# One decoder layer, self attention: the product of weights and values as four 32-column tiles of the array, one per head, with four batches in a group and one copy out of PSUM

## The chip, the cores and the metric

The kernel runs on one core of a Trainium2 chip. The core has five engines that run side by side and wait for one another through semaphores: TensorE (matrix products; PE in the profile, with its weight loads as PEld), VectorE (DVE), ScalarE (ACT), GpSimd (POOL) and SyncE (SP), which here only issues DMAs. Products come out in PSUM, in banks [...], and a DVE or ACT instruction has to copy them to SBUF.

The metric is the device time of one execution in microseconds (us). Three runs of the kernel before took 1482.58, 1488.05 and 1488.45 us; the median, 1488.05, is the time before. Shorter is better.

## What is computed

A decoder layer for 16 batches of 100 tokens, width 512: causal self attention with 16 heads of 32, a residual and a layer norm; cross attention to 361 encoder tokens; a layer of eight experts. The change touches the end of the self attention only:

```python
score = jnp.einsum('bhqd,bhkd->bhqk', q, k) * scale
score = jnp.where(mask, -jnp.inf, score)
attn = jax.nn.softmax(score, axis=-1)
o = jnp.einsum('bhqk,bhkd->bhqd', attn, v)
o = o.transpose(0, 2, 1, 3).reshape(b, s, H)
return o @ w_o.T
```

The line with `attn, v` is the one that is computed in another way. For one batch and one head it is a product of 100x100 weights with 100x32 values.

## The kernel before

**Tiling.** The 16 batches are taken in four groups `g` of `GB` = 4 batches; `r` is the batch in its group. The 512 columns (16 heads) are taken in four chunks `c` of 128 columns, which are four heads; `j` is the head in its chunk. An item is one `(g, c, r)`: four heads of one batch. There are 64 items, and 16 pairs `(g, c)`.

**Work of an item.** `self_scores` (L323) makes the scores of four heads in one bank (three products in float32r, since a float32 number is held as a pair of float32r numbers: `mm3`, L129), adds the mask and takes the minimum on DVE (L332), takes the exponential on ACT (L350, or L343 and L346), and scales by the inverse sum on POOL (L360). `self_turn` (L367) transposes the four 100x100 blocks with TensorE (L372) into a bank of tag `t`, and ACT copies them to `pT` (L374), so that the key token is on the partitions. `self_attend` (L376) then multiplies: the stationary operand is `v`, 100 key tokens by the 128 columns of the chunk; the moving operand is all of `pT`, 100 by 400 (four heads side by side). This product is in float32. Its result `av` is 128x400, and of every head's 100 columns only the 32 rows of that head are wanted, a diagonal of four 32x100 blocks. Four copies bring these blocks to `O`, on DVE (L389) or on ACT (L391). After the fourth batch a DMA on SP's queue writes `O` to DRAM (L393), from where the output projection `b_load` reads it later.

**Order.** A loop over the 64 items (L475 to L482) calls `self_attend` of item i, then what `extra` puts there (the projections of the next chunk: `self_q`, `self_k`, `self_v`, each 12 products; weight loads; the first tiles of the output projection), then the scores of item i + 3 and the transposes of item i + 1. A scheduler takes these calls and sets each engine's final order by a timeline of its own; buffers of pools set what can be in flight: `v` has 6, `pT` has 2, `av` has 2 banks.

**After it.** The output projection and the queries of the cross attention follow (`b_out`, `b_q`). The queries' weights `wq_2` and `wq_3` are loaded near the end of the self attention into the arena slots of the self attention's own weights; their DMAs (L189) stand on SP's queue behind the output DMA (L393) of the last group.

Of the kernel before, what the change touches and what calls it, by code (L numbers as in the profile page):

```python
# [17 lines left out]
B, S, D = 16, 100, 512  # batches, tokens of a batch, model width  # L18
T = B * S
KC = D // 128  # chunks of the model width  # L20
NH = 16  # heads of both attentions
HD1 = D // NH  # head width of the self attention
SE = 361  # encoder tokens of a batch
SP = SE + 1  # the same, even
NKV, HD2 = 4, 128  # key/value heads and head width of the cross attention
GR = NH // NKV
CH = [(0, 128), (128, 128), (256, SE - 256)]  # chunks of the encoder tokens
NE = 8  # experts
GB = 4  # batches of a token group
NG = B // GB  # L30
GT = GB * S
TT = [(t, min(128, T - t)) for t in range(0, T, 128)]  # tiles of all tokens
# [5 lines left out]
def pieces(t0, n):  # L38
    """The batches that tokens t0 to t0 + n lie in: (batch, its token, offset, count)."""
    out, t = [], t0  # L40
    while t < t0 + n:
        b, r = divmod(t, S)
        m = min(S - r, t0 + n - t)
        out.append((b, r, t - t0, m))
        t += m
    return out


class Pair:
    """A float32 array as the exact sum of two that float32r holds."""  # L50
# [12 lines left out]
def tile_decoder_layer(  # L63
# [29 lines left out]
    # Exp and Ln of one table serve both attentions.  # L93
# [25 lines left out]

    def split(dst, src, high=None, low=None):  # L120
        """dst, a pair, from src."""
        high, low = high or nc.scalar, low or nc.vector
        if high is nc.scalar:
            nc.scalar.copy(dst.h, src)  # L124
        else:
            high.tensor_copy(dst.h, src)
        low.tensor_tensor(dst.l, src, dst.h.bitcast(FP), ALU.subtract)  # L127

    def mm3(out, a, b, start, stop):  # L129
        """The product of two pairs, to float32's accuracy."""  # L130
        nc.tensor.matmul(out, a.h, b.h, start=start, stop=False)  # L131
        nc.tensor.matmul(out, a.h, b.l, start=False, stop=False)  # L132
        nc.tensor.matmul(out, a.l, b.h, start=False, stop=stop)  # L133
# [5 lines left out]
    def rsqrt(v, p, n, name, p_=None):  # L139
        """1 / sqrt(v), from the activation tables, with one Newton step."""  # L140
# [33 lines left out]
    # Eight slots of 512 rows by 512 columns, each a pair: weights, and what fits  # L174
    # beside them.
# [9 lines left out]
    def split_rows(dst, src, name, high=None, low=None):  # L185
        """Weights from DRAM into a pair, by rows."""
# [48 lines left out]
    def chunk(n, c, queue=None):  # L235
        """Weights from DRAM, 128 columns (of queries or keys) or rows (of values)."""
# [18 lines left out]
    # Keys of four heads, each in its own block of rows and of columns.  # L255
# [8 lines left out]
    # Added to negated scores: zero up to the diagonal, BIG past it.  # L264
# [25 lines left out]
    def self_v(g, r):  # L290
# [6 lines left out]
        V[g, r] = w1.tile([S, D], FP, name=f"v_{g}_{r}", tag="v", bufs=6)  # L297
        nc.scalar.copy(V[g, r], pv)

    def self_q(g, c):  # L300
# [3 lines left out]
        # The scores come out negated and scaled.  # L304
# [62 lines left out]
    def self_turn(g, c, r):  # L367
# [5 lines left out]
        PT[g, c, r] = w2.tile([S, 4, S], FP, name=f"pT_{n}", tag="pT")  # L373
        nc.scalar.copy(PT[g, c, r], pt)  # L374

    def self_attend(g, c, r):  # L376
        n = f"{g}_{c}_{r}"
        cols = slice(r * S, (r + 1) * S)
        pT = PT.pop((g, c, r))
        # Of each head's rows only its own columns are its output.  # L380
        av = bank("av", [128, 4, S], f"av_{n}")
        v = V[g, r][:, c * 128 : (c + 1) * 128]
        nc.tensor.matmul(av, v, pT, start=True, stop=True)  # L383
        if r == 0:
            O[g, c] = w2.tile([128, GT], FP, name=f"o_{g}_{c}", tag="o")
        for j in range(4):
            rows = slice(32 * j, 32 * j + 32)
            if j == 3 or (j == 1 and r % 2 == 0):
                nc.vector.tensor_copy(O[g, c][rows, cols], av[rows, j, :])  # L389
            else:  # L390
                nc.scalar.copy(O[g, c][rows, cols], av[rows, j, :])  # L391
        if r == GB - 1:
            nc.sync.dma_start(o1d[g][:, c], O[g, c])  # L393

# [34 lines left out]
    LA = 3  # items that scores are ahead by  # L429
    extra = {}  # what comes with an item  # L430
# [44 lines left out]
    for i, it in enumerate(items):  # L475
        self_attend(*it)
# [4 lines left out]
        if i + 1 < len(items):  # L481
            self_turn(*items[i + 1])  # L482
    a_l.close()

# [23 lines left out]
    # Both norms' weights and the negated scale of the scores.  # L508
# [107 lines left out]
    # Six pairs of values and two of queries, in slots 1 and 5.  # L616
# [87 lines left out]
    def x_attend(b, g, i):  # L704
# [13 lines left out]
        # The weights of a token sum to one: the values' bias comes last.  # L718
# [27 lines left out]
    TAIL = 3  # tiles whose parts come by weights, not by tiles  # L746
# [12 lines left out]
    def d_part(i, among={}):  # L759
        """A part of the output's product; others' products are among its own."""  # L760
        t, g = parts[i]
        n = TT[t][1]
        if g == 0:
            # The scores' banks are free by the time that those of the first wait.
# [28 lines left out]
    HEAD = 1  # parts with a group of heads of the last batch  # L793
# [51 lines left out]
    # Small products: logits, ranks, counts, tokens of slots, their experts.  # L845
# [30 lines left out]
    def d_logits(t):  # L876
        """The products of the router with a tile, to go among longer ones."""
# [15 lines left out]
    # An expert's tokens in order, 128 to a tile of slots. The tiles of slots come in  # L893
    # the order in which their first tokens do, but the first EARLY of those that the
    # tokens of the first CUT tiles fill come before the others.
    URGENT = 1000
    I32, HF = mybir.dt.int32, mybir.dt.float16
    NSL = NE + (2 * T - NE) // 128  # tiles of slots: enough for any choice
    CUT, EARLY = NT - 4, 11
    # At the cut at most NE - 1 tiles' worth of choices lies in tiles not full.  # L900
# [9 lines left out]
    # Whole numbers below 2 ** 11 are in float16 where products take them.  # L910
    # Expert numbers less NE, negative ones.
# [5 lines left out]
    # Ones where the partition's number comes before the column's.  # L917
# [11 lines left out]
    # lower[e, i] is one where i is less than e, on all partitions.  # L929
# [31 lines left out]
    def by_128(dst, src, name):  # L961
        """The whole part of src / 128."""
# [5 lines left out]
    def table(name, shape, dt=FP):  # L968
        """A table of shape, first after partitions the tiles."""
# [3 lines left out]
    def choose(a, b):  # L973
        """The two experts of each token of tiles a to b, and its ranks in them."""
# [4 lines left out]
        for j in range(2):  # L979
            # The largest value of each token, and the first place that has it.  # L980
# [19 lines left out]
        if b == NT:  # L1000
            # The last tile's tokens past the end choose none.
# [17 lines left out]
        if b in (CUT, NT):  # L1019
            # The choices that come before each tile of tokens.  # L1020
# [26 lines left out]
        # What the tokens give to their slots: the tile's expert, by its first slot,  # L1047
# [7 lines left out]
        # and their numbers.  # L1055
# [11 lines left out]
    def settle(a, b):  # L1067
        """The tiles of slots of the choices of tiles a to b."""
# [6 lines left out]
        # Tiles of slots that an expert has before each tile of tokens.  # L1075
# [4 lines left out]
        # One where it opens another.  # L1080
# [5 lines left out]
        def before_it(these, till, less, name):  # L1086
            """How many of these come before each."""
# [28 lines left out]
        # That one's place among all tiles of slots.  # L1116
        new = before_it(opn, opened, EARLY if a else 0, "new")
        if a == 0:
# [6 lines left out]
            # new less those of the first EARLY that come before it, negated,  # L1125
# [3 lines left out]
            # or first, if it is itself of those.  # L1129
# [6 lines left out]
        # The place of the one before it.  # L1136
# [7 lines left out]
        # The tile of slots of a choice, by its rank.  # L1144
# [18 lines left out]
    def slots(a, b, upto):  # L1163
        """Of tiles a to b of slots: the tokens, and where the weights lie."""
# [69 lines left out]
    early = [1, 2, 5, 6]  # slots that are free already  # L1234
# [117 lines left out]
    # Tiles of tokens from REST on come after the last product, from LATE on also  # L1352
    # the gathers for them.
    REST, LATE = 6, 8
    # When the tiles before LATE are turned to, by tiles of slots.
    TURN = (19, 20, 21, 22, 24, 26, 28, 30)
    BEHIND = 2  # products that the last norms come after

    def upto(t):
        """Tiles of slots among which are all that the tokens of tile t are in."""  # L1360
        # At most NE of the tiles so far are not full at the cut.
# [93 lines left out]
    # Roots taken together: of tiles in the first norm, of tiles in the second.  # L1455
# [16 lines left out]
    def root(j, t, of=V2):  # L1472
        """What to take the root of for tile t in norm j, or its reciprocal root."""
# [8 lines left out]
    def f_first(t):  # L1482
        """The first norm of tile t, and what the second takes."""
# [3 lines left out]
        # The first norm's result and x2, both times the root s: the second norm  # L1487
        # drops s, but for its share of v.
# [62 lines left out]
    def roots(v, m, name):  # L1551
        """Of v's first m columns the root of four times it, of the others 1 / sqrt."""
# [6 lines left out]
        # A Newton step for each.  # L1559
# [15 lines left out]
    def newton(v, name):  # L1575
        """1 / sqrt(v): from a guess by v's exponent, three Newton steps."""
# [130 lines left out]
```

## Time and profile before

The profiled execution has a span of 1484.0 us, from its first instruction to its last; some 4 us lie around it when it is set beside the median of 1488.05 us. The self attention takes the first 257 us of the span.

| in the first 257 us of the span | instructions | busy us | mean ns of one |
|---|---|---|---|
| TensorE, all products | 1194 | 239.3 | |
| product av (L383) | 128 | 56.1 | 534 |
| transposes pt (L372) | 256 | 32.9 | 257 |
| VectorE, all | 835 | 177.9 | |
| ScalarE, all | 626 | 183.5 | |
| GpSimd, all | 159 | 140.4 | |
| ScalarE copy pT (L374), 100x400 | 64 | 30.6 | 487 |

How to read it: a float32 product of the program shows as two products, each with a weight load of its own, so the 64 products at L383 are 128 rows; a transpose shows as one, so four transposes for each of the 64 items are 256 rows. The mean duration of a product is not its price, since products are pipelined: a product lasts until its last result is out, while the next has long begun. The price is the distance between starts, and the chain of waits shows it. Busy times of different engines lie beside each other and are not to be added.

### The profile page before, as it was taken

The page shows a single profiled execution, that of the slowest core. Times are in us where ns is not written, and L with a number is a line of the kernel's source. Part 1 is how long each engine was busy: PE and PEld are TensorE (multiplying, and loading weights), DVE is VectorE, ACT ScalarE, POOL GpSimd, SP SyncE. Part 2 cuts the span into 40 slices and gives each one's busy share as a digit, 9 for nine tenths or more (in the row PEclk, how much of TensorE's full clock was granted, in tenths as well). Part 3 has the DMA queues.
Part 4 walks back from the last instruction along what each step waited for, and adds up shares of the span by engine and source line. Part 5 has one row for each costly group of instructions (what it writes and reads, how often), then busy time and mean ns, then how long its engine had stood idle before and what let it go on. Part 6 is the DMA issues. An engine that isn't in the chain of part 4 may idle for free.

```text
span 1484.0 us, 24770 instructions
## 1 busy us (share of the span) xinstructions
PE 1391.4 (94%) x7248; PEld 1139.8 (77%) x7248; DVE 1018.2 (69%) x3523; ACT 813.3 (55%) x2164; POOL 731.9 (49%) x853
## 2 busy tenths in 40 slices
PE   7999999999999999999999999999999898798985
PEld 6777786788877888788788788788887676576763
DVE  5775766677676777777777677677745558752698
ACT  5766877444444566566666566566654233332453
POOL 6455545534424555455655555555544444442643
PEclk9999999999999999999999999999999999899997
DMA  4011015456544222122322322321435645666774
GB/s 130 34 46 62 22 36 145 144 142 118 125 97 92 74 65 80 44 64 64 89 61 64 87 63 63 93 60 45 99 107 142 207 164 159 191 213 184 253 232 146
DMA packets 197875, 159.77 MB, mean 108 GB/s; under 512 B 133322, under 2 KB 152878, under 8 KB 197742
## 3 DMA queue, kind: packets, MB, share of 16 engines
q1 hardware_dynamic: 187904, 137.83, 33.7%
q0 software_dynamic: 4576, 14.95, 3.3%
q10 hardware_dynamic: 5262, 5.41, 1.3%
q8 instruction: 60, 0.98, 0.3%
q14 instruction: 73, 0.60, 0.1%
HBM read 107.16 MB, written 50.99 MB: 107 GB/s over the span
## 4 chain that ended last, share of the span: by engine, by line
PE 67%; DVE 17%; DMA 7%; issue 4%; ACT 3%; POOL 1%; SPq 1%; DVEq 0%; POOLq 0%; ACTq 0%
PE pv L131 4%; PE pv L132 4%; PE pv L133 4%; PE pq L131 4%; PE ptp L700 4%; PE pq L132 4%; PE pq L133 3%; PE s L131 3%; PE s L133 3%; PE s L132 3%; PE pk L131 3%; PE pk L133 3%; PE pk L132 3%; DVE ksq L639 2%; PE av L383 2%
## 5 line engine op out<-in xcount | busy, mean ns | idle before, releaser
L692 POOL TENSOR_SCALAR p<-p,sums 100x361 f32<-100x361 f32 x256 | 146.7, 577 | 107.7 <-DVE sums L691 88.7
L679 DVE CUSTOM_DVE_ANT_0 p<-s,nmask 100x361 f32<-100x361 f32 x256 | 133.5, 527 | 73.6 <-PE s L133 71.5
L690 ACT ACTIVATE p<-p,nm 100x361 f32<-100x361 f32 x256 | 153.4, 602 | 47.2 <-DVE nm L679 44.1
L127 DVE TENSOR_TENSOR pT_l<-ptp,pT_h 128x400 fp32r<-128x400 f32 (+1 forms) x192 | 107.4, 567 | 58.3 <-ACT pT_h L124 58.1
L124 ACT CAST pT_h<-ptp 128x400 fp32r<-128x400 f32 (+1 forms) x192 | 91.5, 488 | 33.4 <-PE ptp L700 32.8
L700 PE MATMUL ptp<-ident,p 100*128 100x100 f32 (+1 forms) x768 | 108.2, 253 | 0.1
L700 PEld LDWEIGHTS ptp<-ident,p 100*128 100x128 f32 (+1 forms) x768 | 95.9, 152 | 15.5 <-POOL p L692 4.2
L127 POOL TENSOR_TENSOR cT_l<-cf,cT_h 128x512 fp32r<-128x512 f32 (+1 forms) x48 | 54.4, 1134 | 97.2 <-ACT cT_h L124 95.9
L133 PE MATMUL acc<-WH,ot_l 128*128 128x512 f32 (+1 forms) x208 | 86.2, 415 | 8.4 <-DVE ot_l L127 5.4
L131 PE MATMUL acc<-WH,ot_h 128*128 128x512 f32 (+1 forms) x208 | 85.8, 413 | 3.5 <-ACT ot_h L124 3.5
L127 POOL TENSOR_TENSOR WL<-qf,WH 128x400 fp32r<-128x400 f32 x64 | 67.3, 1051 | 43.5 <-ACT WH L124 39.7
L131 PE MATMUL s<-kT_h,WH 128*100 128x362 f32 x256 | 88.7, 357 | 0.0
L131 PE MATMUL av<-pT_h,WH 128*128 128x400 f32 (+1 forms) x192 | 76.7, 400 | 8.2 <-ACT pT_h L124 8.2
L132 PE MATMUL acc<-WL,ot_h 128*128 128x512 f32 (+1 forms) x208 | 84.4, 406 | 0.0
L133 PE MATMUL s<-kT_h,WL 128*100 128x362 f32 x256 | 84.1, 329 | 0.0
L132 PE MATMUL s<-kT_l,WH 128*100 128x362 f32 x256 | 83.7, 327 | 0.0
L131 PE MATMUL pq<-WH 128*128 128x512 f32 (+1 forms) x208 | 82.3, 396 | 0.1
L132 PE MATMUL pq<-WL,WH 128*128 128x512 f32 (+1 forms) x208 | 81.6, 394 | 0.5 <-POOL WL L127 0.5
L551 POOL TENSOR_TENSOR qs<-qs,r_q 128x512 f32<-128x512 f32 (+1 forms) x52 | 54.3, 1075 | 54.5 <-DVE r_q L155 25.5
L131 PE MATMUL pv<-WH,cT_h 128*128 128x512 f32 (+1 forms) x192 | 80.3, 418 | 0.8 <-DVE WL L127 0.8
L639 DVE CUSTOM_DVE_ANT_0 ksq<-ks 128x128 f32<-128x128 f32 (+1 forms) x192 | 78.3, 408 | 2.4
L360 POOL TENSOR_TENSOR p<-p,rinv 100x400 f32<-100x400 f32 x64 | 54.2, 855 | 51.8 <-DVE rinv L359 37.3
(349 smaller groups left out, 4407.3 us busy)
## 6 DMA issues: line engine op xcount, KB each, us to landing
qf<-qd SPq DMA_DIRECT2D x64, 200.0 KB, 2.6
of<-od SPq DMA_DIRECT2D x48, 256.0 KB, 3.5
cf<-in_ctxT SPq DMA_DIRECT2D x16, 722.0 KB, 4.2
eb<-in_expert_b SPq DMA_DIRECT2D x32, 256.0 KB, 3.8
ysd<-xs SPq DMA_DIRECT2D x32, 256.0 KB, 4.1
f_e<-in_expert_w SPq DMA_DIRECT2D x30, 256.0 KB, 4.5
f_wq<-in_Wq SPq DMA_DIRECT2D x16, 256.0 KB, 4.0
f_wo<-in_Wo SPq DMA_DIRECT2D x16, 256.0 KB, 4.6
```

The source lines that it names most:

```text
L124: nc.scalar.copy(dst.h, src)
L127: low.tensor_tensor(dst.l, src, dst.h.bitcast(FP), ALU.subtract)
L131: nc.tensor.matmul(out, a.h, b.h, start=start, stop=False)
L132: nc.tensor.matmul(out, a.h, b.l, start=False, stop=False)
L133: nc.tensor.matmul(out, a.l, b.h, start=False, stop=stop)
L360: nc.gpsimd.tensor_tensor(p, p, rinv.unsqueeze(2).to_broadcast([S, 4, S]), ALU.mult)
L551: nc.gpsimd.tensor_tensor(qr[:, hs, :], qr[:, hs, :], rs[:n, hs].unsqueeze(2).to_broadcast([n, GR, HD2]), ALU.mult,)
L639: nc.vector.tensor_tensor_reduce(out=sq[:n], in0=kr[:, h, :], in1=kr[:, h, :], scale=1.0, scalar=0.0, op0=ALU.mult, op1=ALU.add, accum_out ...
L679: nc.vector.tensor_tensor_reduce(out=p, in0=sc[:, :SE], in1=nmask, scale=1.0, scalar=BIG, op0=ALU.add, op1=ALU.min, accum_out=nm,)
L690: nc.scalar.activation(p, p, AF.Exp, bias=nm, scale=-1.0, accum_out=sh)
L692: nc.gpsimd.tensor_scalar(p, p, sh, 1.0, ALU.mult, ALU.mult)
L700: nc.tensor.transpose(pt[:n, h, :], probs[h][:, c0 : c0 + n], ident[:S, :S])
```

## The change

`self_attend` is no longer called for an item but once for a pair `(g, c)`, after the last batch's item. It makes 16 products, one for each batch and head, each with a stationary operand of 32 columns (that head's values) and a moving operand of 100 columns (that head's weights). `tile_position=(0, 32 * j)` places head `j` in the array's columns 32j to 32j + 31, and its result falls on partitions 32j to 32j + 31 of the bank, in the columns of its batch. The bank then holds the output as it is wanted, and one ACT copy of 128x400 takes it to `o`; the DMA is unchanged. The last batch comes first in the order of the products, and `in_turn` fixes that order for the scheduler; it adds no wait on a semaphore. `v` gets 8 buffers and `pT` 6, since weights of four batches are kept until the fourth is there. In the loop the call moves behind the extras, the scores and the transposes.

```diff
+    def in_turn(ins, prev):
+        if prev is not None:
+            tc.add_manual_dep(
+                ins.ins, prev.ins.name,
+                mybir.DependencyInfo(
+                    mybir.DependencyClass.NoSync, mybir.DependencyReason.DATA
+                ),
+                reason="in_turn",
+            )
+        return ins
...
-        V[g, r] = w1.tile([S, D], FP, name=f"v_{g}_{r}", tag="v", bufs=6)
+        V[g, r] = w1.tile([S, D], FP, name=f"v_{g}_{r}", tag="v", bufs=8)
...
-        PT[g, c, r] = w2.tile([S, 4, S], FP, name=f"pT_{n}", tag="pT")
+        PT[g, c, r] = w2.tile([S, 4, S], FP, name=f"pT_{n}", tag="pT", bufs=6)
...
-    def self_attend(g, c, r):
-        n = f"{g}_{c}_{r}"
-        cols = slice(r * S, (r + 1) * S)
-        pT = PT.pop((g, c, r))
-        av = bank("av", [128, 4, S], f"av_{n}")
-        v = V[g, r][:, c * 128 : (c + 1) * 128]
-        nc.tensor.matmul(av, v, pT, start=True, stop=True)
-        if r == 0:
-            O[g, c] = w2.tile([128, GT], FP, name=f"o_{g}_{c}", tag="o")
-        for j in range(4):
-            rows = slice(32 * j, 32 * j + 32)
-            if j == 3 or (j == 1 and r % 2 == 0):
-                nc.vector.tensor_copy(O[g, c][rows, cols], av[rows, j, :])
-            else:
-                nc.scalar.copy(O[g, c][rows, cols], av[rows, j, :])
-        if r == GB - 1:
-            nc.sync.dma_start(o1d[g][:, c], O[g, c])
+    def self_attend(g, c):
+        av = bank("av", [128, GB, S], f"av_{g}_{c}")
+        prev = None
+        for r in (GB - 1, *range(GB - 1)):
+            pT = PT.pop((g, c, r))
+            for j in range(4):
+                h = c * 128 + 32 * j
+                ins = nc.tensor.matmul(
+                    av[32 * j : 32 * j + 32, r, :],
+                    V[g, r][:, h : h + 32],
+                    pT[:, j, :],
+                    start=True,
+                    stop=True,
+                    tile_position=(0, 32 * j),
+                )
+                prev = in_turn(ins, prev)
+        o = w2.tile([128, GT], FP, name=f"o_{g}_{c}", tag="o")
+        nc.scalar.copy(o, av.rearrange("p r s -> p (r s)"))
+        nc.sync.dma_start(o1d[g][:, c], o)
...
     for i, it in enumerate(items):
-        self_attend(*it)
         for f in extra.get(it, []):
             f()
         if i + LA < len(items):
             self_scores(*items[i + LA])
         if i + 1 < len(items):
             self_turn(*items[i + 1])
+        if it[2] == GB - 1:
+            self_attend(*it[:2])
```

Comments and docstrings are also gone from the changed file, which moves its line numbers and nothing else.

More of the change, by code (lines that the diff above doesn't have):

```diff
@@ L118, in pair @@
         )
+    def in_turn(ins, prev):
+        if prev is not None:
+            tc.add_manual_dep(
+                ins.ins,
+                prev.ins.name,
+                mybir.DependencyInfo(
[4 more added lines that the diff above has]
+        return ins
     def split(dst, src, high=None, low=None):
```

## The prediction, made before the changed kernel was run

> **What bounds the kernel now.** First the engines' busy times on the page, then the chain of waits over the stretch that the change touches, then single pieces of that chain, then the groups of the lines concerned.
>
> ```profile
> PE 1391.4 (94%) x7248; PEld 1139.8 (77%) x7248; DVE 1018.2 (69%) x3523; ACT 813.3 (55%) x2164; POOL 731.9 (49%) x853
> ...
> PE 67%; DVE 17%; DMA 7%; issue 4%; ACT 3%; POOL 1%; SPq 1%; DVEq 0%; POOLq 0%; ACTq 0%
> ```
>
> TensorE is busy 94% of the span, and two thirds of the chain that ended last run on it. What it saves mostly arrives at the end; what the others save counts only where the chain passes through them. The same chain, asked for the first 257 us alone, begins so:
>
> ```profile
> by line: PE av L383 12.4%; PE pv L131 5.8%; PE pv L132 5.4%; PE pt L372 5.3%; PE pv L133 5.2%; issue 4.7%; DVE p L332 4.2%; PE pk L131 4.2%; DVE WL L127 4.1%; PE pk L133 3.8%; PE pk L132 3.8%; PE s L131 3.3%; DMA f_wq<-in_Wq 3.3%; PE pq L13
> ```
>
> The product to be changed is its largest line: 12.4% of 257 us, 31.8 us. What one product costs shows in the chain's pieces near 240 us (start, length, what):
>
> ```profile
> 239.75 0.69 PE pt L372 x8
> 240.44 0.26 PE pa L133
> 240.69 1.36 PE av L383 x4
> 242.05 0.02 issue
> 242.07 0.23 ACT o L391
> ...
> 246.77 1.72 PE pt L372 x8
> 248.49 2.71 PE av L383 x4
> ...
> 255.42 5.67 DMA f_wq<-in_Wq
> ```
>
> Two products, four rows of 400 columns, take 1.36 us: 0.34 a row, 0.68 a product. Eight transposes, float32 rows of 100 columns, take 0.69: 0.086 a row. So a row's price follows its moving columns (0.85 ns each). At 246.77 the same work takes twice as long; the granted clock of 246.6 to 253.4 us is 0.51. The copies:
>
> ```profile
> L391 ACT COPY o<-av 32x100 f32<-32x100 f32 x160 | 36.7, 232 | 30.3 <-PE av L383 21.5 <-DVE o L389 6.9
> L389 DVE COPY o<-av 32x100 f32<-32x100 f32 x96 | 24.8, 262 | 21.5 <-ACT o L391 18.9 <-PE av L383 0.6
> L374 ACT COPY pT<-pt 100x400 f32<-100x400 f32 x64 | 30.6, 487 | 1.3 <-PE pt L372 0.7
> ```
>
> A copy costs 232 to 262 ns for 100 elements a partition, and 487 ns for 400: four times the columns for twice the price.
>
> **The products.** All counts are per pair (g, c), of which there are 16. Before: 4 products at 0.68, 2.72 us. After: 16 products of 100 columns, each of two rows, so 32 rows. The moved columns are 32 x 100 = 3,200, as many as 8 x 400 before. One after another they save nothing: 32 x 0.086 = 2.75 us. The gain hangs on tiles that run at the same time, and no row of this trace shows a column tile. The cases:
>
> - All four tiles at once: 4 batches x 2 rows x 0.086 = 0.69 us. But 32 weight loads must be made too. The nearest row is the router's product at L884, which loads 128 columns for only 8 moving ones: eight such rows take 0.95 us of which the last result's 0.26 are its tail, so 0.1 us a load, 0.025 for 32 columns, 0.80 us for all 32. The loads bind: 0.80.
> - In pairs: rows start in program order, which is high part then low part of one head, then the next head's. A head's low part has to follow its high part in the same tile; the next head's high part is another tile and can run beside it. So each product costs one row and not two: 16 x 0.086 + 0.086 = 1.46.
> - One after another: 2.75.
> - One after another with loads uncovered: 32 x (0.086 + 0.025) = 3.55.
>
> Here the Trainium skill has rules for both sides. "TensorE: Matmul & The Clock Gate", Part 3 (The mechanism, and Measured speedup vs the span model), says that packed tiles start about 4 ns apart, a column packing of three measuring 2.38 times; by that rule alone the four tiles cost 0.69 + 16 x 0.004 = 0.75. The same section says that weight loads overlap running products only when row groups differ. Column tiles share all rows, so by that rule the loads lie bare, the fourth case. The trace speaks against this second rule: the transposes also use the same rows, load 100 columns each (0.08 us by the row above) and still start every 0.086 us, not every 0.17. The same section also says that products start and end in strict order, and that is what gives pairs. I take the pairs, since the high and low halves of a float32 product are adjacent in the built program's order on TensorE, and keep 0.80 and 3.55 for the ends.
>
> To each comes entering and leaving the tiled form. "TensorEngine Tiling (Array Packing)", Key Properties, says that a change of mode drains the array, with no price; the nearest row is how long a product outlasts its pace, 0.50 (its median duration) less 0.34, 0.16 us. Twice, 0.33; nothing if the drain is hidden. The built order keeps the 16 products together at nearly all 16 places (one transposition group or one score product cuts in at two), so two switches each. Sums: 1.13, 1.79, 3.08, 3.88 us against 2.72. Times 16: -25.4, -14.9, +5.8, +18.6.
>
> Of the 64 x 0.68 = 43.5 us now spent, 31.8 lie on the chain, 73%. A saving counts in that share: -18.6 or -10.9. A loss I count whole, because work that grows comes onto the chain.
>
> **The copies.** 256 go (36.7 + 24.8 = 61.5 us busy), 16 of 128x400 come at 0.49, 7.8 us, on ACT. Adding the chain's pieces on these lines gives 3.0 us for ACT and 2.9 for DVE, 5.9 of 61.5 busy. The same tenth of 7.8 remains, 0.8: -5.1 us on the chain. The rest of the 54 us saved is beside TensorE's work and gives nothing. Behind each new copy, ACT's next instructions (exponentials, pT copies) queue 0.49 where up to three old copies took 0.7, so that is no loss.
>
> **What is late next.** The first product of a group waits for the last batch's pT. In the built order, 12 projection rows or a few scores and transposes lie between at most places; in the last two groups only four transposes, 0.35 to 0.45 us against ACT's 0.49 copy: about 0.5 us in all. Then the queries' weights: their loads stand on SP's queue behind the output DMA of group (3, 2), take 5.67 us at 255.42, and pass ACT and POOL before TensorE may use them; in the trace TensorE already waits for them near 262 and 264 us. Products that get there up to 1 us sooner only wait longer: 1 us. Together +1.5. More buffers for v and pT take waits away that the list of waits prices at nearly nothing. SP's 16 output DMAs are the same, the POOL work too, and the later stages' built order is the old one but for a few swaps near the end, which I cost at nothing.
>
> **Sum.** -10.9 - 5.1 + 1.5 = -14.5 us: span 1484.0 to 1469.5. With the 4 us around it, which is the median's offset from the span, **1473.5 us**.
>
> **The rivals.**
>
> - *All four tiles run at once.* For it speaks the span rule; against it the order of high and low halves. -18.6 - 5.1 + 1.5 = -22.2: 1466.
> - *The tiles run one after another* (the change doesn't do what it says). For it: column counts are equal, and the switches cost. +5.8 - 5.1 + 1.5 = +2.2: 1490, no change that can be told.
> - *Loads lie bare in the tiled form, slower.* One mechanism, one place, the 16 runs of 32 rows: each row waits for its own load. +18.6 - 5.1 + 1.5 = +15: 1503. It decides as soon as a row costs more than (2.72 - 0.33) / 32 = 0.075 us plus what the copies give back, 3.6 us / 512 rows = 0.007, so from 0.082. One after another with covered loads stands just past that point.
>
> **How the numbers follow.** Chances: pairs 0.48, all at once 0.25, one after another 0.14, bare loads 0.13. What no case holds is the clock: three half-clock stretches (3.4, 6.8 and 6.8 us) lie in the self attention, and one more or less of 6.8 moves the time by 3.4. With it the pairs reach from 1466 to 1482. The range, 1460 to 1495, takes in the pairs, nearly all of four at once and most of one after another. About 0.5% (1480.6 to 1495.5) is what a measurement of this kernel can tell from no change. Faster by more: 0.85 of the pairs, nearly all of the second case, a tenth of the third, 0.66 in all; same 0.20; slower 0.14, bare loads and a little of the third.
>
> **What would show it.** In the changed profile the new product's line should have 512 rows, and a run of 32 should take about 1.5 us on the chain: 0.8 says all at once, 2.8 one after another, 3.5 bare loads. In the window of the first 257 us ACT's busy time should fall by about 29 us and DVE's by 25, and the first product of the queries should start about 15 us before its 254.7. The prediction is wrong if the runs of 32 are as long as the four products were, if TensorE's new idle time meets half-clock stretches, or if the softmax takes the place of the product on the chain, so that shorter runs leave the same start of the queries.

## The result, and the profile after

Four runs of the changed kernel took 1467.66 to 1474.53 us, median **1472.76 us**, beside 1486.59 us for the kernel before (four runs): ratio 0.9911, 95% interval 0.9889 to 0.9933. The forecast was 1473.5. The profiled execution's span is 1472.8 us (before 1484.0). Comments that left the file and a new helper move the lines: what was L372, L374 and L360 is now L385 (transposes), L387 (copy to `pT`) and L373 (scaling of `p`); the product is L398, the copy out L408.

The groups by line and shape, in the first 257 us (busy us, mean ns of one | idle time just before, and what ended it):

```profile
L398 PE MATMUL av<-pT,v 100*32 100x100 f32 x512 | 16.3, 267 | 2.6 <-ACT pT L387 2.6
L408 ACT COPY o<-av 128x400 f32<-128x400 f32 x16 | 7.8, 488 | 7.7 <-PE av L398 7.6
```

The 512 rows and 16 copies are there as counted. What the product costs is read from starts, not from the mean of 267 ns. TensorE's timeline (start us, length us, what), at a place without idle time:

```profile
200.96 0.35 PE L146 MATMUL s<-WH,qT_l 128*100 128x400 f32 x1
201.24 0.89 PE L398 MATMUL av<-pT,v 100*32 100x100 f32 x32
202.06 0.55 PE L385 MATMUL pt<-ident,p 100*100 100x100 f32 x4
```

From the start of the score row before to that of the transposes after are 1.10 us. The score row itself takes 0.18 (its neighbours start 0.18 apart), so the run of 32 rows costs 0.92 us, where the four products cost 2.72. Its 31 distances between starts are, in ns:

```
7, 7, 6, 91, 6, 6, 7, 66, 7, 6, 7, 65, 8, 6, 7, 65, 8, 6, 6, 67, 7, 5, 8, 65, 7, 6, 8, 65, 7, 6, 7
```

Four rows start within 20 ns, and the next four some 86 ns after the first of these (111 the first time), which is the price of one 100-column row. **All four tiles run at once**: 0.65 us from the first start to the last, then 0.18 until the next row, and some 0.1 more than usual at the entry. Twelve of the 16 runs take 0.64 to 0.65 us from first start to last; in two other work cuts in, and two ran in part or whole while the granted clock was 0.5 (1.12 and 1.19 us).

Did the saved time arrive? The first product of the queries (128x512, on TensorE) starts at 242.58 us, before it was 254.71. The busy times of the engines up to these two points (length of the window, then busy us of each engine, granted clock, share of the DMA engines, GB/s), after and before:

```profile
core 0: us, PE busy (x) PEld busy (x) DVE busy (x) ACT busy (x) POOL busy (x), PEclk, DMA share, GB/s
0.00:242.58 242.58, 210.40 (x1568) 176.86 (x1569) 154.28 (x738) 156.44 (x486) 147.29 (x164) 0.95 0.24 75
```

```profile
0.00:254.71 254.71, 236.97 (x1184) 189.57 (x1185) 177.20 (x832) 181.54 (x621) 138.13 (x157) 0.97 0.21 66
```

TensorE is busy 26.6 us less, and idle 32.2 instead of 17.7 us. So of 26.6 us saved, 12.1 arrived, and 14.4 became idle time. Behind this point the kernel takes as long as before: 1230.2 us to the end of the span, before 1229.3. The same two windows, each cut at 200 us, show where:

```profile
0.00:200.00 200.00, 180.52 (x1306) 153.25 (x1307) 126.35 (x614) 128.46 (x401) 117.66 (x135) 0.97 0.19 61
200.00:242.58 42.58, 29.88 (x264) 23.62 (x263) 27.94 (x125) 27.98 (x86) 29.64 (x30) 0.83 0.48 141
```

```profile
0.00:200.00 200.00, 184.66 (x926) 148.86 (x927) 135.77 (x623) 138.27 (x466) 110.16 (x127) 0.97 0.19 60
200.00:254.71 54.71, 52.31 (x260) 40.71 (x259) 41.43 (x212) 43.27 (x155) 27.97 (x31) 0.94 0.30 88
```

Up to 200 us TensorE is idle 19.5 us (before 15.3); in the tail, from there to the first query product, 12.7 of 42.6 us (before 2.4 of 54.7). About 4 of the 14 us lie in the first stretch and 10 in the tail. TensorE's timeline there:

```profile
226.12 0.89 PE L398 MATMUL av<-pT,v 100*32 100x100 f32 x32 [0.25 <-ACT pT L387]
230.46 0.55 PE L385 MATMUL pt<-ident,p 100*100 100x100 f32 x4 [3.45 <-POOL p L373]
231.28 0.77 PE L385 MATMUL pt<-ident,p 100*100 100x100 f32 x4 [0.26 <-POOL p L373]
236.97 0.91 PE L385 MATMUL pt<-ident,p 100*100 100x100 f32 x4 [4.92 <-POOL p L373]
...
240.32 1.56 PE L398 MATMUL av<-pT,v 100*32 100x100 f32 x32 [1.59 <-ACT pT L387]
```

The brackets hold the idle time ahead of a row and its releaser. The last items' weights (`p`) come late from GpSimd, which waits for DVE's sums of the exponentials. ScalarE's timeline shows one reason:

```profile
225.58 0.88 ACT L387 COPY pT<-pt 100x400 f32<-100x400 f32 x2
230.53 0.62 ACT L137 CAST WH<-f_wq 128x512 fp32r<-128x512 f32 x1 [4.07 <-DMA f_wq<-in_Wq]
...
232.46 0.53 ACT L359 ACTIVATE p<-p 100x400 f32<-100x400 f32 x1
...
239.26 0.62 ACT L137 CAST WH<-f_wq 128x512 fp32r<-128x512 f32 x1 [5.10 <-DMA f_wq<-in_Wq]
239.78 0.49 ACT L387 COPY pT<-pt 100x400 f32<-100x400 f32 x1
```

ScalarE stands 4.07 and 5.10 us at casts of the queries' weights, whose transfers have not landed; behind the first stands the last item's exponential, behind the second the last copy of `pT`, for which the last product waits. This is not the only reason: TensorE's gap of 3.45 us ends at 230.46, before the first of these casts has begun, so this gap does not come from it.

### The profile page after: what moved, and what is told of

Same layout as the page of the kernel before. It is cut to its first block, busy times and chain, and to the rows that moved or that the text cites. A ratio compares the mean times of both kernels' runs of the same rounds, so it can differ in the third digit from the quotient of the medians.

```text
span 1472.8 us, 25211 instructions
## 1 busy us (share of the span) xinstructions
PE 1366.8 (93%) x7632; PEld 1130.0 (77%) x7632; DVE 998.5 (68%) x3427; ACT 784.2 (53%) x2020; POOL 733.3 (50%) x853
## 5 line engine op out<-in xcount | busy, mean ns | idle before, releaser
L717 PEld LDWEIGHTS ptp<-ident,p 100*128 100x128 f32 (+1 forms) x768 | 95.9, 152 | 15.4 <-POOL p L709 4.2
L144 PE MATMUL pk<-WH,cT_h 128*128 128x512 f32 (+1 forms) x192 | 77.4, 403 | 0.7 <-DVE ks L647 0.7
```

The source lines that it names most:

```text
L717: nc.tensor.transpose(pt[:n, h, :], probs[h][:, c0 : c0 + n], ident[:S, :S])
```

## The experiments

Twelve kernels were run. In the table, "first query product" is its start, and TensorE's busy time is that up to it; the rest up to it is idle time. They were measured in four sets, each with its own runs of the kernel before, whose medians were 1488.05 (after_again to old_product_late), 1484.00 (wq3_late to quarter_product), 1484.74 (wq2_early to before_wq2_early) and 1485.70 us (both_late), so kernels of different sets are set beside each other by their ratios. The last two columns come from one profile each. How far such values scatter shows in the two profiles of the changed kernel: the query products start at 242.58 and 243.70 us, and the part behind them takes 1230.2 and 1238.2 us.

| kernel | median us | ratio to before (95% interval) | first query product us | TensorE busy, idle us |
|---|---|---|---|---|
| before | 1486.59 | 1 | 254.71 | 237.0, 17.7 |
| after_again | 1473.76 | 0.9901 (0.9867 to 0.9935) | 243.70 | 208.9, 34.8 |
| heads_outer | 1485.96 | 0.9988 (0.9975 to 1.0001) | 255.99 | 228.4, 27.6 |
| small_copies | 1475.96 | 0.9925 (0.9901 to 0.9950) | 242.13 | 209.3, 32.9 |
| old_product_late | 1499.91 | 1.0079 (1.0052 to 1.0106) | 263.40 | 236.3, 27.1 |
| wq3_late | 1469.02 | 0.9872 (0.9834 to 0.9910) | 240.01 | 211.5, 28.5 |
| wq_own_queue | 1473.85 | 0.9898 (0.9855 to 0.9941) | 234.88 | 209.3, 25.6 |
| casts_pool | 1475.95 | 0.9920 (0.9889 to 0.9952) | 243.99 | 209.7, 34.3 |
| quarter_product | 1477.24 | 0.9924 (0.9894 to 0.9955) | 246.62 | 205.0, 41.7 |
| wq2_early | 1473.47 | 0.9932 (0.9908 to 0.9956) | 240.79 | 212.5, 28.3 |
| wq2_early_late | 1471.11 | 0.9901 (0.9878 to 0.9923) | 239.75 | 211.8, 28.0 |
| before_wq2_early | 1500.64 | 1.0092 (1.0066 to 1.0118) | 263.88 | 236.2, 27.7 |
| both_late | 1471.32 | 0.9930 (0.9906 to 0.9955) | 241.93 | 210.9, 31.1 |

### What each part of the change is worth

**after_again** is the changed kernel once more; its profile gives the chain of waits of this stretch, which the first one does not.

> The changed kernel once more, for a chain of waits and as the level for the runs beside it. All theories: ratio to before 0.991 (0.989 to 0.993), the 32 product rows of a run in groups of four starts 6 to 8 ns apart, groups 86 ns apart.

The chain from 215 us on (start, length, what), from a layer norm's step to the last product:

```profile
221.64 4.84 DVE t_ln L160
226.89 0.56 DVE xr L180
227.46 0.33 SPq L442
227.84 0.42 SPq L202
228.32 4.25 DMA f_wq<-in_Wq
232.60 0.62 ACT WH L137
...
234.97 1.46 DVE xr L180
236.45 0.33 SPq L442
236.82 0.43 SPq L409
237.36 3.00 DMA f_wq<-in_Wq
240.41 0.50 issue
240.91 0.49 ACT pT L387
241.44 1.56 PE av L398 x32
```

It goes round: a layer norm on DVE ends in `xr`; SyncE's queue has waited for it to store `x1d` (L442); behind this store stand the weights' transfers (L202); ScalarE waits for them, and the next layer norm waits for ScalarE (`y_ln`). The product holds 9.2 us of the chain up to 250 us, where the products of before had 31.8 up to 257; the transfers of `f_wq` hold 11.0, where they had 8.5 before (3.3% of 257).

**heads_outer** makes all batches of one head, then the next head, so that eight rows in a row use one tile:

```diff
-        for r in (GB - 1, *range(GB - 1)):
-            pT = PT.pop((g, c, r))
-            for j in range(4):
+        pTs = [PT.pop((g, c, r)) for r in range(GB)]
+        for j in range(4):
+            for r in (GB - 1, *range(GB - 1)):
...
-                    pT[:, j, :],
+                    pTs[r][:, j, :],
```

> The same 16 products and the same copy, but head by head: all four batches of head 0, then head 1, so that eight rows in a row stand in the same column tile. Theory A (the gain of the product is that different tiles run at the same time): rows of one tile start 86 ns apart, a run of 32 takes about 2.6 us instead of 0.65, 1.9 us more for each of 16 runs, 30 us of TensorE; the time rises by 15 to 30 us, ratio to before 1.001 to 1.011. Rival B (a row with a 32-column stationary operand is cheap by itself, whatever stands beside it): run length and time as in the changed kernel, ratio 0.991.

TensorE's timeline of one run, and below it its distances between starts in ns (their sum, from first start to last, is 1.746 us; it is 1.745 in the median run):

```profile
203.13 2.00 PE L398 MATMUL av<-pT,v 100*32 100x100 f32 x32 [0.80 <-ACT pT L387]
```

```
111, 85, 86, 85, 7, 79, 32, 54, 32, 54, 31, 86, 6, 79, 30, 56, 30, 57, 29, 86, 6, 80, 30, 55, 30, 56, 31, 85, 86, 87, 85
```

The same work with only its order changed gives the gain back: 1.745 us a run, and 12.2 us more than after_again in the same set, less than the 15 to 30 expected. That the rows are merely cheap is out; the gain is tiles at the same time. The run is shorter than 2.6 us because neighbouring heads still overlap: only the first five rows and the last few start 86 ns apart (the second 111 ns after the first), and in between they come in twos (30 and 56, or 7 and 79 ns). If a tile's rows go at this pace and the next head begins with the fifth row of the one before, 0.374 us after that head began, the run takes 3 x 0.374 for three heads and 0.626 for the eight rows of the last, 1.75 us, which is what is seen. The durations of the rows show the same: 28 rows of this run last 248 to 250 ns and four last 273, the 1st, 6th, 14th and 22nd to start, at 0, 374, 748 and 1121 ns, one for each head. In the changed kernel's run above, the four rows of 273 ns are the first four, 6 to 7 ns apart. So the long row looks like the first on its tile, and there all four tiles begin together.

**small_copies** has the new product, and the old 16 copies instead of the one:

```diff
-        nc.scalar.copy(o, av.rearrange("p r s -> p (r s)"))
+        for r in range(GB):
+            for j in range(4):
+                rows = slice(32 * j, 32 * j + 32)
+                dst = o[rows, r * S : (r + 1) * S]
+                if j == 3 or (j == 1 and r % 2 == 0):
+                    nc.vector.tensor_copy(dst, av[rows, r, :])
+                else:
+                    nc.scalar.copy(dst, av[rows, r, :])
```

> The tiled products, but 16 copies of 32x100 out of the bank as before (10 on ScalarE, 6 on VectorE) in place of one of 128x400. Theory A (products carry most of the gain, copies 5 us of it): ratio 0.994 to 0.996. Rival C (the relief of ScalarE and VectorE carries the gain): ratio 0.998 to 1.003.

The time is 2.2 us more than after_again's at the median, with overlapping intervals, and the queries start no later. The ratio, 0.9925, lies below the 0.994 to 0.996 of Theory A: the copies are worth less than the 5 us put on them. ScalarE and DVE are busy 28 and 21 us longer (184.37 and 177.33 us up to the first query product, against 156.27 and 156.41 in after_again), but the start of the queries does not show it.

**old_product_late** has the later call and the buffers, but per batch the old product and its copies:

```diff
-                ins = nc.tensor.matmul(
-                    av[32 * j : 32 * j + 32, r, :],
...
+            av = bank("av", [128, 4, S], f"av_{g}_{c}_{r}")
+            v = V[g, r][:, c * 128 : (c + 1) * 128]
+            nc.tensor.matmul(av, v, pT, start=True, stop=True)
...
```

> The call stays behind the fourth batch and the buffers stay at 8 and 6, but each batch is multiplied as before, 128 columns by 400, each into its own bank with the old four copies. Theory A: the product costs 2.7 us a group again, copies too, and the tail of the self attention still waits: ratio 1.000 to 1.010. Rival D (the gain comes from the later call and the deeper buffers, not from tiles and copy): ratio 0.991 to 0.995.

It is slower than before, by 11.9 us. With all four products of a pair in one place and two `av` banks, TensorE waits for the copies out of them:

```profile
251.42 3.04 PE L396 MATMUL av<-pT,v 100*128 100x400 f32 x4 [2.32 <-DVE o L401]
257.51 1.70 PE L396 MATMUL av<-pT,v 100*128 100x400 f32 x2 [3.05 <-DVE o L401]
```

TensorE waits 18.2 us for DVE's copies ahead of this product up to the queries, before 2.9. The two kernels are steps from before to after. By medians of this set: the later call and buffers +11.9 us (1488.05 to 1499.91), the product -24.0 (to 1475.96), the one copy -2.2 (to 1473.76). The first two are no prices of single things: the tiled product puts four batches into one bank, so its step also takes away the wait for banks that the step before had brought.

### What took the idle time

Theory 1: the weights' transfers, in front of the last exponentials and copies, took the gain back. Theory 2: the last items' own chain through four engines ends there, and a wait that is removed lays bare another.

**wq3_late** calls the load of `wq_3` two items later, so that its casts stand behind the last exponential:

```diff
-    at(last, 3, 1, load_unit, "wq_3", 1, Wqg[3])
+    at(last, 3, 3, load_unit, "wq_3", 1, Wqg[3])
```

> The load of the wq_3 weights is called at the last item of the self attention, (3,3,3), and not at (3,3,1); all else is as after the change. In after, ScalarE's queue stands at two casts of these weights (4.07 and 5.10 us for f_wq to land) with the last exponentials and copies of pT behind them, and PE has 8.9 us of work between 220 and 240 us. Theory 1 (the product's gain is taken back because ScalarE waits for these weights ahead of the last exponentials): the first query product comes 4 to 9 us earlier than the 242.6 to 243.7 us of after, and the kernel takes 1464 to 1470 us, unless the wq_3 products at about 250 us then wait for their weights. Theory 2 (the idle is the chain of scores, GpSimd's subtract, exponential and GpSimd's product of the last items, whatever stands in ScalarE's queue): the first query product stays within 1.5 us and the time within 2 us of after's 1473.

**wq_own_queue** starts the transfers of `wq_2` and `wq_3` from GpSimd (`q=nc.gpsimd` in both calls of `load_unit`, handed to `split_rows`):

```diff
-            tc.keep_in_program_order(nc.sync.dma_start(f, src[:, k]))
+            tc.keep_in_program_order((q or nc.sync).dma_start(f, src[:, k]))
```

> The transfers of wq_2 and wq_3 are started by GpSimd and not by SyncE, where they stand behind loads that wait 11.2 us for olp_l, 6.5 us for xr and 9.2 us for o; the casts stay on ScalarE. Theory 1: with the weights there in time, ScalarE's waits of 9.2 us for f_wq shrink to under 3 us, the first query product comes 4 to 8 us earlier than after's 242.6 to 243.7, and the kernel takes 1465 to 1470 us. Theory 2 (the last items' own chain sets the end): ScalarE's wait shrinks too, but PE's idle moves to the wait for GpSimd's p, and the time stays within 2 us of 1473; GpSimd's issuing of eight transfers delays p by 1 us or so each and may make it slower, up to 1480.

**casts_pool** casts these weights on GpSimd:

```diff
-    at(last, 2, 3, load_unit, "wq_2", 0, Wqg[2])
+    at(last, 2, 3, load_by_pool, "wq_2", 0, Wqg[2])
...
-    at(last, 3, 1, load_unit, "wq_3", 1, Wqg[3])
+    at(last, 3, 1, load_by_pool, "wq_3", 1, Wqg[3])
```

> The high halves of wq_2 and wq_3 are cast by GpSimd and not by ScalarE. Theory 1 (ScalarE's block is what holds the last exponentials): ScalarE no longer waits for f_wq and the exponentials go ahead, but GpSimd, which makes p itself, has eight more casts of over 1 us; the gain and the cost nearly cancel, 1468 to 1478 us. Theory 2 (the last items' chain through GpSimd sets the end): GpSimd's casts stand ahead of the last p and the time rises to 1478 to 1485 us.

**quarter_product** keeps the products of one batch in four:

```diff
             pT = PT.pop((g, c, r))
+            if r != GB - 1:
+                continue
             for j in range(4):
...
-        nc.scalar.copy(o, av.rearrange("p r s -> p (r s)"))
+        nc.scalar.copy(
+            o.rearrange("p (r s) -> p r s", s=S),
+            av[:, GB - 1 : GB, :].to_broadcast([128, GB, S]),
+        )
```

> Three quarters of the products of weights and values are left out: of each group of four batches only the last one's four tile products run, and the copy spreads them over the four batches. 8 rows are left of 32. If the product as it stands is nearly gone from the path (theory 1: what is left of the path is other engines' chain), the first query product moves by under 3 us from 242.6 to 243.7, and its 9 us in the chain of waits shrink to about 4 with others taking their place. If every us of the product still counts (theory 2), 16 x 24 rows x 22 ns = 8.3 us go, and the first query product comes at about 235 us. The whole time may move otherwise, since the tokens' values, and with them the experts' loads, are others.

quarter_product is the clearest. Its window up to the first query product:

```profile
0.00:246.62 246.62, 204.96 (x1185) 168.51 (x1185) 157.32 (x738) 157.26 (x486) 147.03 (x164) 0.94 0.24 74
```

TensorE is busy 4 to 5 us less than in after, and the queries start 3 to 4 us later. What is left of the product buys nothing there. From heads_outer to after_again, 16 x (1.745 - 0.645) = 17.6 us of product were worth 12.2 us; the next 5 us are worth none.

wq_own_queue had the earliest queries, 7.7 and 8.8 us ahead of the two runs of after, and no gain in time. For the start of the queries this is what Theory 1 expected. The stretch after that point shows why the time did not follow, with the transfer's issue and the row that ends the stall:

```profile
234.88:260.00 25.12, 21.47 (x88) 17.08 (x87) 10.41 (x18) 8.02 (x15) 11.30 (x12) 0.92 0.56 181
```

```profile
237.99 0.55 POOL L202 DMA_DIRECT2D f_wq<-in_Wq  x1
...
245.69 0.79 PE L144 MATMUL pq<-WH 128*128 128x512 f32 x1 [3.53 <-ACT WH L137]
```

The last transfers now stand behind GpSimd's own work: this one is issued at 237.99 us, its cast begins at 245.02, and the queries wait for their weights. wq3_late gains 2.6 and 3.7 us at the queries' start, short of the 4 to 9 of Theory 1 and more than the 1.5 of Theory 2. It had the lowest time of all, 1469.02, in the span of Theory 1, but its interval overlaps with those of after, so that it is faster than after is not shown. casts_pool changes nothing at the start of the queries, and its time lies in Theory 1's span and not in the slower one of Theory 2. small_copies bears on this too: there ScalarE waits only 0.25 and 0.93 us for `f_wq` in the tail, and the queries start at 242.13 us all the same.

**wq2_early** loads `wq_2` 11 items earlier into the slot that the value weights have left, and `wq_3` where `wq_2` was; **wq2_early_late** loads `wq_3` at the last item; **before_wq2_early** is the first of the two in the kernel before:

```diff
-    at(last, 2, 3, load_unit, "wq_2", 0, Wqg[2])
+    at(last, 0, 3, load_by_pool, "wq_2", 2, Wqg[2])
+    at(last, 2, 3, load_unit, "wq_3", 0, Wqg[3])
-    at(last, 3, 1, load_unit, "wq_3", 1, Wqg[3])
-            load_unit("wk", 2, kp(Wk))
+            load_unit("wk", 1, kp(Wk))
-    spare = [slot_of(s)[:, k] for s in (1, 5) for k in range(KC)]
+    spare = [slot_of(s)[:, k] for s in (2, 5) for k in range(KC)]
```

> After's product, with the load of wq_2 moved 11 items of the self attention earlier: at (3,0,3), by GpSimd, into the weights' slot 2, which the value weights have left by then; wq_3 takes its place at (3,2,3) and slot 0, and nothing is loaded at (3,3,1); the cross attention's wk and spare slots change places. Half of the f_wq transfers thus leave the tail. Theory 1 (late f_wq transfers, standing behind SyncE's stores of x1d and in front of ScalarE's last exponentials and pT copies, took the product's gain back): the wait of ScalarE for f_wq between 220 and 245 us falls from 9 to 15 us to under 4 us, the first query product comes at 232 to 238 us instead of 242.6 to 243.7, with PE's idle up to it near 25 us, the query products then don't wait for weights, and the time is 1461 to 1467 us. Theory 2 (the last items' chain of scores, subtract, exponential and scaling sets the end by itself): PE's waits for GpSimd's p stay, the first query product stays after 240 us, and the time stays within 3 us of 1473.

> As wq2_early, with wq_3 called at the last item (3,3,3), so that its casts also stand behind the last exponentials. Theory 1: the first query product is as early as in wq2_early or 1 to 3 us earlier, but the fourth query product of the first tile may wait for wq_3; time 1460 to 1468 us, within 3 us of wq2_early. Theory 2: as for wq2_early, within 3 us of 1473.

> The same move of the wq_2 and wq_3 loads in the kernel before, with its old product. Theory 1 (before, the tail was bound by PE's own work, and its f_wq casts stood behind the exponentials): little to gain, 0 to 5 us of the 1484 to 1488; the early loads are then worth more with the new product than without it. If they gain as much here as there (8 us or more), then the weights' lateness is a fault of both kernels alike and not what took the product's gain back.

ScalarE's wait for `f_wq` from 200 us on is down to 2.0 us in wq2_early and 3.4 in wq2_early_late, as Theory 1 wanted, yet the idle time falls only to 28 us, the queries start 2 to 4 us earlier, and the total stays where it was, as Theory 2 expected. Part of the idle time moved ahead: in wq2_early TensorE is busy 15.4 us of the slice from 200 to 220 us, where after has 18.8. In the kernel before, the same move costs 9 us at the queries' start and 15.9 in time, which neither theory had expected; idle there rises from 17.7 to 27.7. Why was not followed up.

**both_late** is wq3_late with the first two stores of `x1d` moved behind the transposes that read the same `xr`, which breaks the link from L442 to L202 in the chain above:

```diff
-        nc.sync.dma_start(x1d[t][:n], xr[:n])
+        if t > 1:
+            nc.sync.dma_start(x1d[t][:n], xr[:n])
...
+        if t < 2:
+            nc.sync.dma_start(x1d[t][:n], x1[:n])
         X1T[t] = slot_of(7)[:, t % KC].rearrange("p (k n) -> p k n", n=128)
```

> wq3_late (the wq_3 load called at the last item) with one more edit: the stores of x1d for the first two token tiles are started after the transposes that read the same xr, and not right after the layernorm, so that in SyncE's queue two f_wq transfers come ahead of the loads that wait for olp_l and ahead of the store that waits for xr, and all four ahead of the second store. Theory 1 (the tail's idle in after is f_wq behind SyncE's waits, as in the chain of the repeated run: xr, store, f_wq 4.25 us, cast, then xr, store, f_wq 3.00 us, cast, pT copy): the first query product comes 2 to 6 us earlier than the 240.0 us of wq3_late, at 234 to 238 us, and the time is 1462 to 1468 us. Theory 2 (each wait removed in the tail lays bare another of about the same length): the first query product stays within 2 us of wq3_late's, PE's idle up to it stays at 26 to 30 us, and the time stays at 1466 to 1472 us.

ScalarE's two waits for `f_wq` at 231.93 and 233.11 us are down to 0.20 and 0.17 us, and the queries start at 241.93, later than in wq3_late. Its chain shows what came in place of the transfers:

```profile
232.75 3.49 DVE xr L180
236.24 0.49 DVE sums L360
237.07 0.86 POOL p L373
237.98 0.91 PE pt L385 x4
```

The last sum of the softmax on DVE stands behind a layer norm step that takes 3.49 us, and GpSimd's scaling and TensorE's transposes stand behind the sum. That favours Theory 2, as wq2_early and wq2_early_late do (the idle time here, 31.1 us, is even above its 26 to 30): the wait for the weights was real in after, and removing it alone brings little in time. wq_own_queue, with its earlier start, does not fit it, so neither theory is shown. One more candidate stands untested. The 14 DVE instructions of the tail's two layer norms take 4.6 us in before, 8.6 in after, 10.7 in after_again and 12.2 in both_late; they stand in the chain, and the last section shows one of them stretched beside GpSimd. No kernel kept GpSimd away from them, so their share is not known. Which of the waits in the tail would have to go together is not settled.

## Why the prediction was right, point by point

The time was met within 0.8 us, but this was luck: two large errors of opposite sign cancelled. That the gain comes from tiles at the same time was right; how many, and how much of it arrives, was not.

- **The products.** I took pairs (1.79 us, -10.9 on the chain); it is all four at once, the first rival. The step that failed is "products start and end in strict order, and that is what gives pairs", together with the order of high and low halves: four starts within 20 ns can't be both halves of one head in one tile, since heads_outer shows such rows 86 to 111 ns apart. The starts look as if rows of a free tile pass up to three waiting rows; the trace does not name the tile of a row, so this is inferred from starts and durations. A run costs 0.92 us, less even than the rival's 1.13: all 32 rows start within 0.65 us, so that the loads, put at 0.80, do not bind, and entering and leaving cost some 0.1 us each and not 0.33 together. On TensorE that is 16 x (2.72 - 0.92) = 28.8 us saved, where the prediction had 14.9. In time the step measured -24.0 instead of -10.9, from the slower kernel old_product_late.
- **The share on the chain.** 73% of 43.5 us as a rule for every saved microsecond was a fair slope for the first part (heads_outer to after_again: 12.2 of 17.6, 69%), but no rule to the end: quarter_product shows the slope at zero. With the measured 28.8 us the prediction's own sum would have been -21.0 - 5.1 + 1.5 = -24.6, 1463 us; the 9 us that are missing are about what the tail's idle time grew by, 10.3.
- **The copies.** -5.1 expected, -2.2 measured between the medians. Their busy time fell by less than the 29 and 25 us said for the first 257 us: ScalarE's by 23.4 and DVE's by 18.6, since this window now holds 14 us of the next stage; up to the first query product it is 25.1 and 22.9.
- **What is late next.** +1.5 expected; beside the products this is the term most mis-sized. With the new product the idle time up to the queries is 14.4 us longer. (The later call and buffers cost +11.9 with the old product, waits for its banks included.) I had counted the 0.5 us at the last `pT` and 1 us for the weights after the first query product, but not that ScalarE's queue holds the weights' casts ahead of the last exponentials, so that a faster TensorE runs into them; they are one wait among several.
- **The rivals.** One after another (1490) and bare loads (1503) fall: the 31 distances show neither. Of the signs of being wrong, the last, that the softmax takes the product's place on the chain, came true in part.
- **The clock**, another of these signs, came true as well, but does not explain the gain that is missing: 11.1 us of after's tail, from 231.5 us to the first query product, are at a granted clock of 0.50, and 6.5 of the tail's 12.7 idle us lie in them. Up to that product TensorE is busy for 18.2 us at half clock, before for 15.8, so at half speed the difference can have cost some 1.2 us.
- **The mark for the first query product** (15 us earlier) came out at 12.1.

## What to carry to other kernels

Here four column tiles taken in turn, head by head within a batch, ran at once, four rows in the 86 ns of one; the same products ordered tile by tile took 2.7 times as long from first start to last. Size the gain in two steps: what the engine saves, and how much of it the other engines can follow. Leave out most of the shortened work once, to see whether it still counts before tuning it further, and expect a change of place to have a price of its own: here it cost 12 us with the old product and its two banks.

## What was not expected of the hardware

- High and low halves that are adjacent in the program don't hold the tiles apart: rows start 6 to 7 ns after each other in fours, and the fours 85 to 87 ns after each other (the second 111).
- A DVE instruction of one column a partition took 4.83 us. In after_again, DVE's timeline and GpSimd's beside it:

```profile
221.64 4.83 DVE L160 SCALAR_TENSOR_TENSOR t_ln<-y_ln,v_ln 128x1 f32<-128x1 f32 x1 [1.45 <-ACT y_ln L157]
226.50 0.15 DVE L166 TENSOR_SCALAR t_ln<-t_ln 128x1 f32<-128x1 f32 x1
```

```profile
221.51 0.86 POOL L356 TENSOR_TENSOR p<-p,nm 100x400 f32<-100x400 f32 x1
222.32 1.67 POOL L373 TENSOR_TENSOR p<-p,rinv 100x400 f32<-100x400 f32 x2
223.94 1.28 POOL L140 TENSOR_TENSOR WL<-f_wq,WH 128x512 fp32r<-128x512 f32 x1
225.17 1.28 POOL L140 TENSOR_TENSOR olp_l<-ol,olp_h 128x512 fp32r<-128x512 f32 x1
```

The shortest of this line takes 0.20 us. This one ends at 226.47, with the end of five GpSimd instructions that follow each other without a gap (226.45). "SBUF — State Buffer" of the Trainium skill has, in its section on the two separate sides of SBUF, an exclusive lock on a port pair that VectorE and GpSimd share, taken by DVE instructions with two SBUF inputs among others. The rows agree with it, and show more than a wait for one instruction: DVE did not get in between the five. In the first profile of the same kernel this instruction took 1.23 us, and the queries started within 1.1 us of the same time, so this one wait is not what sets the tail.
